# Layer 2 of a four-layer convolution kernel: the last half image cut in two quarters, and the half before it measured by ScalarE sums that GpSimd folds

## The chip, the cores and the metric

The kernel runs on one core of one Trainium2 chip. A core has a matrix engine (TensorE, PE in the profile, with its weight loads shown apart as PEld), a vector engine (VectorE, DVE), a scalar engine (ScalarE, ACT), GpSimd (POOL), and a queue engine (SyncE, SP) that issues transfers. Each engine works through its own list of instructions in order, and waits on semaphores for the others. The metric is the device time of one execution in microseconds. Before the change the median of three runs is 950.27 us (950.23 to 951.56).

## The reference, cut to what matters

The input is 16 images of 256 channels and 28 x 28 pixels. Four layers follow one another; the change is in layer 2, which consists of two binary convolutions with batch normalisations:

```python
out = batchnorm(x, g1, b1); out = binact(out)          # signs
out = prelu(binconv(out, w1, 1), a1)                   # first convolution, "l2b" below
out = batchnorm(out, g2, b2); out = binact(out)
out = prelu(binconv(out, w2, 1), a2)                   # second convolution, "l2c" below
out = batchnorm(out, g3, b3)
out = prelu(out + x, a3)
```

`batchnorm` takes the mean and the variance of each channel over all 16 images. So nothing behind such a normalisation can start before the last pixel of the last image has been convolved, activated and counted. Layers 0 and 1 come before (a binary convolution; a Winograd-like convolution with gates), layer 3 after (attention over the 784 pixels of each image).

## The kernel before, in words

The 256 channels are two groups of 128 partitions, called `mo` or `k` (0 and 1). An image is 784 values per partition and group; half an image is 14 rows, 392 values (`HN`), and a quarter is 7 rows, 196 values. Weights are plus and minus one. Two output channels are packed into one weight (`PACK`), so that one matmul computes both groups, and the result is split afterwards.

`sign_layer` (line 358) runs a binary convolution over a list of blocks `(image, first row, rows)`. Layer 2 uses `HALVES`, 32 blocks of 14 rows; layer 0 uses `PARTS`, which is the same list with its last block cut into two quarters of 7 rows. The order is written out by hand for PE, ACT, DVE and SP; GpSimd's instructions, and everything outside those blocks, are ordered by a planner. For block j it issues:

- `products(j)`: 18 matmuls (2 input groups x 3 rows x 3 columns of the kernel window) into one PSUM tile, line 378.
- the signs of the next image (ScalarE, line 1206), when a new image begins.
- `post(j-1)`: the activation and statistics of the block before, see below.
- `apart(j)`: ScalarE takes the packed product out of PSUM as int16 (line 394), and VectorE subtracts it to get the other channel (line 396). This pair waits for the matmuls of block j.
- the work that `post(j-1)` returned for ScalarE (`after`).

`post2.post` (line 1230) treats one block for the groups `mo` = 1 and 0. VectorE applies PReLU (line 1241) into the resident tile `pt`, and then collects count, mean and squared deviation with a statistics instruction (line 1249). For group 1 of every second of the first 22 blocks (`EARLY`), `by_sums` says that there is no statistics instruction: the PReLU instruction also gives the sum, and ScalarE gives the sum of squares around a base value (`square_p`, line 1260). Besides this, ScalarE squares the raw values for a range guard (`square`, line 1254, "doubts"); those of the last image are kept in `last_squares` and issued by `late_squares` after the layer.

`Moments` holds the statistics. `gather` (line 177) aggregates the first 22 blocks early; its result goes into the first three columns of `fin`. Each later block has six columns of `fin`, which VectorE fills. At the end a call (line 209) aggregates `fin` once per group. Then `sign_norm` (line 244, after l2b) or `norm` (line 212, after l2c) makes scale and shift of them with some ten tiny VectorE instructions and one square root on ScalarE.

After each convolution the code issues `keep_busy(n)` (line 476): n matmuls of 128x512 on a tile of zeros, which nobody reads. They are put into PE's list between the last real matmul and the next real one. Layer 2 uses 30 of them after l2b (line 1298) and 39 after l2c (line 1313). Behind those after l2b come the first matmuls of l2c, which need the signs of image 0 (ScalarE). Behind those after l2c come the first query and key matmuls of layer 3 (line 1454), which need image 0 normalised, added to the residual and activated (lines 1601 to 1608).

GpSimd has little to do around there: when the weights of l2b are no longer needed, it clears a tile of keys in their place (line 1417), and when l2c is over, it clears a few small tiles (lines 1410 to 1417).

Of the kernel before, what the change touches and what calls it, by code (L numbers as in the profile page):

```python
# [27 lines left out]
F32 = mybir.dt.float32  # L28
# [5 lines left out]
AF = mybir.ActivationFunctionType  # L34
ALU = mybir.AluOpType
# [4 lines left out]
P = 128  # L40
B = 16
S = 28
N = S * S
HN = N // 2
# [3 lines left out]
HALVES = [(j // 2, HR * (j % 2), HR) for j in range(2 * B)]  # L48

PARTS = HALVES[:-1] + [(B - 1, r, HR // 2) for r in (HR, HR + HR // 2)]  # L50
NB = len(PARTS)
IMAGES = [(i, 0, S) for i in range(B - 2)]
EARLY = 22
MC = 112
GN, GC = N // 4, MC // 4
NC_ = N // MC
# [29 lines left out]
def forward(ctx: ExitStack, tc: tile.TileContext, d: dict, out: bass.AP, careful: bool):  # L86
# [3 lines left out]
    nc = tc.nc  # L90
    V, A, T = nc.vector, nc.scalar, nc.tensor

    const = ctx.enter_context(tc.tile_pool(name="const", bufs=1))
    wpool = ctx.enter_context(tc.tile_pool(name="wpool", bufs=1))
    small = ctx.enter_context(tc.tile_pool(name="small", bufs=3))
# [7 lines left out]
    def pv(name):  # L103
        return vec[:, VECS.index(name), :]
# [20 lines left out]
    doubts = const.tile([P, 4 * NB + 10], F32, name="doubts")  # L125
# [9 lines left out]
    def tt(o, a, b, op):  # L135
        V.tensor_tensor(o, a, b, op)  # L136
        return o
# [17 lines left out]
    class Moments:  # L155


        def __init__(self, name, early, late, early_count, summed=False):
            self.parts = const.tile([P, 2, early, 6], F32, tag="parts", name=name + "_parts")
            self.summed = summed  # L160
            if summed:
                self.sums = const.tile([P, 2, early // 2], F32, tag="sums", name=name + "_sums")
                self.tot, self.base = (const.tile([P, n], F32, name=name + q) for n, q in ((3, "_tot"), (1, "_base")))
            self.fin = const.tile([P, 2, 3 + 6 * late], F32, name=name + "_fin")
            self.mv = const.tile([P, 2, 2], F32, name=name + "_mv")
            self.early, self.count, self.name = early, float(early_count), name

        def part(self, at, k):
            if at >= self.early:
                return self.fin[:, k, 6 * (at - self.early) + 3:][:, 0:6]  # L170
            return self.parts[:, k, at // 2 if self.summed and k == 1 else at, :]

        def by_sums(self, at, k):

            return self.summed and k == 1 and at < self.early and at % 2 == 1

        def gather(self):

            nc.gpsimd.memset(self.fin[:, :, 0:1], self.count)
            ps = [self.parts[:, k].rearrange("p c s -> p (c s)") for k in range(2)]  # L180
            if self.summed:
                h = self.early // 2
                t, tot, n = self.parts[:, 1, h, :], self.tot, float(h * HN)
                nc.gpsimd.memset(t[:, 0:1], n)
                V.tensor_reduce(tot[:, 0:2], self.sums, AX.X, ALU.add)
                V.tensor_scalar(t[:, 1:2], tot[:, 0:1], 1.0 / n, None, ALU.mult)
                tt(tot[:, 2:3], t[:, 1:2], self.base, ALU.add)
                tt(tot[:, 2:3], tot[:, 2:3], tot[:, 2:3], ALU.mult)
                V.scalar_tensor_tensor(t[:, 2:3], tot[:, 2:3], -n, tot[:, 1:2], ALU.mult, ALU.add)
                ps[1] = ps[1][:, 0:6 * h + 3]  # L190
            for k in range(2):
                V.bn_aggr(self.fin[:, k, 1:3], ps[k])
            V.tensor_scalar(self.fin[:, :, 2:3], self.fin[:, :, 2:3], self.count, None, ALU.mult)
# [160 lines left out]
    def first_part(block):  # L354

        return 2 * block[0] + (block[1] >= HR) + (block[1] > HR)
# [93 lines left out]
    def block_moments(name, blocks, summed=False):  # L450
        return Moments(name, EARLY, len(blocks) - EARLY, EARLY * HN, summed and not careful)

# [15 lines left out]
    with tc.tile_pool(name="ps_conv", bufs=3, space=PSUM) as psc, \  # L468
# [7 lines left out]
        def keep_busy(n):  # L476

            ps = pss.tile([P, 512], F32, tag="sm", name="unused")
            for _ in range(n):
                tc.keep_in_program_order(T.matmul(ps, lhsT=idle[:, 0:P], rhs=idle, start=True, stop=True))  # L480

        with tc.tile_pool(name="ph1", bufs=1) as ph:

            fpads = sign_pads(ph, "vs") if careful else sign_pads(const, None)
# [19 lines left out]
            def temp(tag):  # L504
                return ph.tile([P, HN if careful else N], F32, tag=tag, name=tag, bufs=2)
# [134 lines left out]
            w2a = packed_weights(wpool, tag="wa2")  # L640
# [7 lines left out]
            steps = [constants]  # L648
# [16 lines left out]
            mom = block_moments("l0", PARTS)  # L665
# [521 lines left out]
        with tc.tile_pool(name="ph2", bufs=1) as ph:  # L1187
# [37 lines left out]
            def post2(order, alpha, mom, doubt):  # L1225

                if careful:
                    beta = combine(mom.name + "_beta", alpha, -1.0, 1.0)

                def post(block, ab):  # L1230
                    i, r0, rows = block
                    at = first_part(block)
                    for mo in (0, 1) if careful else (1, 0):
                        y = ab[:, mo]
                        p = pt[order[i]][:, mo, r0 * S:(r0 + rows) * S]
                        if careful:
                            r = temp("t1")[:, :rows * S]
                            A.activation(r, y, AF.Relu, scale=-1.0)
                            V.scalar_tensor_tensor(p, r, beta[:, mo:mo + 1], y, ALU.mult, ALU.add)
                        else:  # L1240
                            V.scalar_tensor_tensor(  # L1241
                                p, y, alpha[:, mo:mo + 1], y, ALU.mult, ALU.max,
                                accum_out=mom.sums[:, 0, at // 2:at // 2 + 1] if mom.by_sums(at, mo) else None,
                            )
                        if mom.by_sums(at, mo):
                            by_sums = p
                            continue
                        for h, _, m in pieces(block):
                            V.bn_stats(mom.part(at + h, mo), p[:, h * HN:h * HN + m * S])
                        if mom.summed and (at, mo) == (0, 1):  # L1250
                            V.tensor_scalar(mom.base, mom.part(0, 1)[:, 1:2], -1.0, None, ALU.mult)

                    def square(h, m):
                        A.activation(
                            temp("t2")[:, :m * S], ab[:, 0, h * HN:h * HN + m * S], AF.Square, scale=SAFE**-0.5,
                            accum_out=doubt[:, at + h:at + h + 1],
                        )

                    def square_p():
                        A.activation(  # L1260
                            temp("t2")[:, :rows * S], by_sums, AF.Square, bias=mom.base,
                            accum_out=mom.sums[:, 1, at // 2:at // 2 + 1],
                        )

                    squares = [lambda h=h, m=m: square(h, m) for h, _, m in pieces(block) if not careful]
                    if mom.by_sums(at, 1):
                        squares.append(square_p)
                    if i < B - 1:
                        return squares
                    last_squares.extend(squares)  # L1270
                    return ()
                return post

            last_squares = []
# [15 lines left out]
            shifted = None  # L1290
            if not careful:
                shifted = ph.tile([P, 2, 2, S + 2, S + 2], SIGNS, name="shifted")
            mom = block_moments("l2b", HALVES, True)
            sign_layer(fpads, w2a, temp, room2, sign2a, post2(order, pv("a1"), mom, doubts[:, 2 * NB:3 * NB]), steps, mom, HALVES,
                       shifted=shifted, direct=4)
            late_squares()

            keep_busy(30)
            sg2, bg2 = sign_norm("l2b", mom, pv("g2"), pv("b2"), sf1)

            mom = block_moments("l2c", HALVES, True)
            sign_layer(
                fpads, w2b, temp, room2, lambda i, rows, out: sign2(pt[i], sg2, bg2, rows, out),
                post2(range(B), pv("a2"), mom, doubts[:, 3 * NB:4 * NB]), [], mom, HALVES, shifted=shifted,
            )
            late_squares()

            if careful:
                keep_busy(45)
                sg3, bg3 = norm("l2c", mom, pv("g3"), pv("b3"), sf2)  # L1310
                tt(bg3, bg3, cc, ALU.add)
            else:
                keep_busy(39)
                with tc.manual_schedule(engines={ET.DVE, ET.Activation}):
                    sg3, shift3 = norm("l2c", mom, pv("g3"), pv("b3"), sf2, late=True)
                    bg3 = shift3(b3c)
# [597 lines left out]
```

## Time and profile before

| what | value |
|---|---|
| median of three runs | 950.27 us |
| the profiled execution: time of its own | 949.96 us |
| its span, first to last instruction | 948.2 us |
| granted TensorE clock | 0.998 |
| busy: PE / DVE / ACT / POOL | 932.7 / 758.2 / 672.6 / 136.4 us |
| end of l2b, ScalarE begins to take out the last block | 558.93 us |
| first matmul of l2c | 565.21 us |
| end of l2c, ScalarE begins to take out the last block | 661.24 us |
| first matmul of layer 3 | 669.73 us |

Times inside the execution are microseconds from the start of the span. Engine times overlap; PE is busy nearly throughout, and in its busy time the unused matmuls of `keep_busy` are counted as well. The two stretches from 558.93 to 565.21 and from 661.24 to 669.73 are the ones in which the change takes place; in both of them PE does nothing that enters the result.

### The profile page before, as it was taken

The page shows a single profiled execution, that of the slowest core. Times are in us where ns is not written, and L with a number is a line of the kernel's source. Part 1 is how long each engine was busy: PE and PEld are TensorE (multiplying, and loading weights), DVE is VectorE, ACT ScalarE, POOL GpSimd, SP SyncE. Part 2 cuts the span into 40 slices and gives each one's busy share as a digit, 9 for nine tenths or more (in the row PEclk, how much of TensorE's full clock was granted, in tenths as well). Part 3 has the DMA queues.
Part 4 walks back from the last instruction along what each step waited for, and adds up shares of the span by engine and source line. Part 5 has one row for each costly group of instructions (what it writes and reads, how often), then busy time and mean ns, then how long its engine had stood idle before and what let it go on. Part 6 is the DMA issues. An engine that isn't in the chain of part 4 may idle for free.

```text
span 948.2 us, 14936 instructions
## 1 busy us (share of the span) xinstructions
PE 932.7 (98%) x5602; PEld 581.8 (61%) x5608; DVE 758.2 (80%) x1436; ACT 672.6 (71%) x1165; POOL 136.4 (14%) x145
## 2 busy tenths in 40 slices
PE   8999999999999999999999999999999999999996
PEld 4555678888888878887555555555444444444442
DVE  4777798999998899987788878889656768687765
ACT  6665568888888888865777756775766666676652
POOL 2001100000000000000000000000334353534431
PEclk9999999999999999999999999999999999999999
DMA  9888434445543444421555201111232434434212
GB/s 349 297 294 269 158 121 139 169 176 204 191 139 139 154 155 158 168 78 60 221 209 211 109 38 60 79 78 59 35 68 68 109 97 91 114 77 128 68 69 105
DMA packets 39332, 130.68 MB, mean 138 GB/s; under 512 B 4866, under 2 KB 16324, under 8 KB 39252
## 3 DMA queue, kind: packets, MB, share of 16 engines
q1 hardware_dynamic: 33332, 98.31, 28.9%
q0 software_dynamic: 5632, 30.54, 11.9%
q8 instruction: 45, 0.74, 0.3%
q10 hardware_dynamic: 288, 0.80, 0.2%
q14 instruction: 35, 0.29, 0.1%
HBM read 72.67 MB, written 32.11 MB: 111 GB/s over the span
## 4 chain that ended last, share of the span: by engine, by line
PE 95%; ACT 1%; DVE 1%; DMA 1%; SPq 1%; issue 0%; DVEq 0%; ACTq 0%
PE cv L378 30%; PE cv L784 29%; PE sc L1477 9%; PE av L1498 8%; PE cv L911 5%; PE mi L1454 5%; PE sm L1540 2%; PE unused L480 2%; PE mi L1558 2%; PE sm L1498 1%; DMA xs<-in_x_dram 1%; PE gate L879 1%; PE hid L687 1%; ACT es L1481 0%; SPq L271 0%
## 5 line engine op out<-in xcount | busy, mean ns | idle before, releaser
L784 PE MATMUL cv<-vs,w 128*128 128x392 f32 (+1 forms) x1296 | 272.5, 352 | 0.3 <-DVE vs L136 0.3
L378 PE MATMUL cv<-fpads,wpk 128*128 128x392 f16 (+1 forms) x1434 | 248.0, 329 | 1.2 <-DVE wpk L303 0.8
L378 PEld LDWEIGHTS <-wpk 128*128 128x128 f16 x1746 | 169.0, 97 | 124.3 <-issue 2.4
L784 PEld LDWEIGHTS cv<-vs,w 128*128 128x128 f32 x768 | 143.2, 190 | 6.2
L1481 ACT ACTIVATE es<-sc 128x784 f32<-128x784 f32 x112 | 87.3, 822 | 41.7 <-PE sc L1477 41.7
L784 PEld LDWEIGHTS <-w 128*128 128x128 f16 x768 | 69.4, 99 | 51.9 <-issue 9.1
L1477 PE MATMUL sc<-q,keyswa 64*128 64x392 f32 x448 | 89.9, 513 | 0.9 <-ACT es L1481 0.9
L1498 PE MATMUL av<-es,v 128*64 128x392 f32 x448 | 80.7, 499 | 0.0
L1241 DVE SCALAR_TENSOR_TENSOR p<-ab,vec 128x392 f32<-128x392 int16 x128 | 77.3, 616 | 0.0
L394 ACT ACTIVATE ab<-cv 128x392 int16<-128x392 f32 x64 | 31.8, 496 | 57.4 <-PE cv L378 54.5
L1491 POOL TENSOR_TENSOR sum<-sum,es 128x784 f32<-128x784 f32 x32 | 67.2, 2100 | 3.1 <-ACT es L1481 0.6
L1477 PEld LDWEIGHTS sc<-q,keyswa 64*128 64x128 f32 x448 | 38.9, 186 | 44.0 <-issue 17.1
L378 PE MATMUL cv<-shifted,wpk 128*128 128x392 f16 x312 | 60.2, 328 | 0.0
L784 PE MATMUL cv<-one_on,w 128*128 128x392 bf16 x240 | 59.5, 329 | 0.0
L1465 DVE COPY keyswa<-mi 64x392 f32<-64x392 f32 x31 | 16.3, 564 | 53.4 <-ACT q L1461 53.4
L1498 PEld LDWEIGHTS av<-es,v 128*64 128x64 f32 x448 | 29.4, 136 | 47.3 <-issue 47.0
L939 POOL DMA_DIRECT2D x2d<-x x16 | 8.6, 537 | 345.3 <-DVE x L933 284.9
L396 DVE SCALAR_TENSOR_TENSOR ab<-ab,cv 128x392 int16<-128x392 int16 x64 | 35.7, 558 | 27.8 <-ACT ab L394 27.5
L766 ACT CAST vs<-vs 128x840 fp32r<-128x840 bf16 x63 | 54.1, 883 | 2.5 <-DVE vs L136 2.5
L911 PE MATMUL cv<-z,fw 128*128 128x392 f32 x256 | 48.9, 342 | 0.1
L911 PEld LDWEIGHTS cv<-z,fw 128*128 128x128 f32 x256 | 46.1, 188 | 0.9 <-ACT z L903 0.9
L1454 PE MATMUL mi<-p,wqk 128*128 128x392 f32 x124 | 45.1, 506 | 0.1
(313 smaller groups left out, 1527.9 us busy)
## 6 DMA issues: line engine op xcount, KB each, us to landing
xs<-in_x_dram SPq DMA_DIRECT2D x30, 784.0 KB, 5.0
one_on<-vs SPq DMA_DIRECT2D x60, 209.8 KB, 3.0
x2d<-x POOLq DMA_DIRECT2D x16, 784.0 KB, 3.6
out_dram<-p SPq DMA_DIRECT2D x15, 784.0 KB, 3.7
shifted<-fpads SPq DMA_DIRECT2D x26, 449.8 KB, 2.7
p<-x2d POOLq DMA_DIRECT2D x14, 784.0 KB, 6.9
p<-x2d SPq DMA_DIRECT2D x13, 784.0 KB, 5.4
n0d<-n POOLq DMA_DIRECT2D x16, 392.0 KB, 4.4
```

Source lines behind the costliest of these rows:

```text
L378: T.matmul(pss[j][:, n // size if careful else h, :rows * S].rearrange("p (a b) -> p a b", b=S), lhsT=w[:, n, c, :], rhs=src[:, blocks[j][ ...
L394: A.activation(by_halves(ab[:, 1], blocks[j]), ps, AF.Copy, scale=1.0 / PACK)
L396: V.scalar_tensor_tensor(a, b, -PACK, ps, ALU.mult, ALU.add)
L766: copy(v, w)
L784: T.matmul(ps.rearrange("p (a b) -> p a b", b=S), lhsT=w[:, k, c, u, mo * P:(mo + 1) * P], rhs=one_on[:, u, k, :, 0:S] if moved and c == 1 ...
L911: T.matmul(ps[:, h, :HN], lhsT=w[:, k, mo * P:(mo + 1) * P], rhs=z2[b][:, k, h * HN:(h + 1) * HN], start=(k + i == 0), stop=(k + i == 2),)
L1241: V.scalar_tensor_tensor(p, y, alpha[:, mo:mo + 1], y, ALU.mult, ALU.max, accum_out=mom.sums[:, 0, at // 2:at // 2 + 1] if mom.by_sums(at, ...
L1454: T.matmul(ps[:, h, :HN], lhsT=wqk[:, k, :], rhs=x[b][:, k, h * HN:(h + 1) * HN], start=(k == 0), stop=(k == 1))
L1477: T.matmul(ps[:, h, :HN], lhsT=chunk[rows], rhs=qs[b][rows], start=True, stop=True)
L1481: A.activation(e, ps[:, :, :HN], AF.Exp, scale=0.125)
L1491: (V if late else nc.gpsimd).tensor_tensor(sums[b, late], sums[b, late], e, ALU.add)
L1498: T.matmul(ps[64 * h:64 * h + 64, :HN], lhsT=w, rhs=e[:, h, :], start=start, stop=stop)
```

## The change

Layer 2 now uses `PARTS`: its last block, 14 rows, becomes two quarters of 7 rows (numbers 31 and 32). The block ahead of them, the first half of the last image (number 30, `LATE`), gets no statistics instructions on VectorE. In their place, for both groups, the PReLU instruction gives a sum, and ScalarE squares the block around `base` with a sum (`square_p`), now issued right after the first quarter has been taken out. A new method `fold` makes count, mean and squared deviation of the four sums with six instructions on GpSimd, and puts them into columns 3 to 5 of `fin`. The base value is kept for both groups, and made after block 0 in one instruction. The unused matmuls are 26 in place of 30, and 35 in place of 39.

```diff
+LATE = 2 * B - 2
...
+                self.tot = const.tile([P, 3], F32, name=name + "_tot")
+                self.base = const.tile([P, 2, 1], F32, name=name + "_base")
+                self.late_sums = const.tile([P, 2, 2], F32, name=name + "_late")
-            self.fin = const.tile([P, 2, 3 + 6 * late], F32, name=name + "_fin")
+            self.fin = const.tile([P, 2, (0 if summed else 3) + 6 * late], F32, name=name + "_fin")
...
             if at >= self.early:
-                return self.fin[:, k, 6 * (at - self.early) + 3:][:, 0:6]
+                n = 6 * (at - self.early) + (3 if not self.summed else 6 if at < LATE else 0)
+                return self.fin[:, k, n:n + 6]
...
-            return self.summed and k == 1 and at < self.early and at % 2 == 1
+            return self.summed and (at == LATE or k == 1 and at < self.early and at % 2 == 1)
+        def sums_at(self, at, k):
+            if at == LATE:
+                return [self.late_sums[:, q, k:k + 1] for q in range(2)]
+            return [self.sums[:, q, at // 2:at // 2 + 1] for q in range(2)]
+        def fold(self):
+            g, n = nc.gpsimd, float(HN)
+            t, d = self.fin[:, :, 3:6], small.tile([P, 2], F32, tag="mv", name="fold")
+            (s, q), base = (self.late_sums[:, i] for i in range(2)), self.base[:, :, 0]
+            g.memset(t[:, :, 0:1], n)
+            g.tensor_scalar(t[:, :, 1], s, 1.0 / n, None, ALU.mult)
+            g.tensor_tensor(d, t[:, :, 1], base, ALU.add)
+            g.tensor_tensor(d, d, d, ALU.mult)
+            g.tensor_scalar(d, d, -n, None, ALU.mult)
+            g.tensor_tensor(t[:, :, 2], d, q, ALU.add)
...
-                                accum_out=mom.sums[:, 0, at // 2:at // 2 + 1] if mom.by_sums(at, mo) else None,
+                                accum_out=mom.sums_at(at, mo)[0] if mom.by_sums(at, mo) else None,
                             )
                         if mom.by_sums(at, mo):
-                            by_sums = p
+                            by_sums.append((mo, p))
                             continue
...
-                        if mom.summed and (at, mo) == (0, 1):
-                            V.tensor_scalar(mom.base, mom.part(0, 1)[:, 1:2], -1.0, None, ALU.mult)
+                        if mom.summed and (at, mo) == (0, 0):
+                            V.tensor_scalar(mom.base, mom.parts[:, :, 0, 1:2], -1.0, None, ALU.mult)
...
-                    def square_p():
+                    def square_p(mo, p):
                         A.activation(
-                            temp("t2")[:, :rows * S], by_sums, AF.Square, bias=mom.base,
-                            accum_out=mom.sums[:, 1, at // 2:at // 2 + 1],
+                            temp("t2")[:, :rows * S], p, AF.Square, bias=mom.base[:, mo], accum_out=mom.sums_at(at, mo)[1],
                         )
...
-                    if mom.by_sums(at, 1):
-                        squares.append(square_p)
+                    squares_p = [lambda s=s: square_p(*s) for s in by_sums]
                     if i < B - 1:
-                        return squares
+                        return squares + squares_p
                     last_squares.extend(squares)
-                    return ()
+                    return squares_p + [mom.fold] if at == LATE and squares_p else ()
...
-            mom = block_moments("l2b", HALVES, True)
+            mom = block_moments("l2b", PARTS, True)
...
-            keep_busy(30)
+            keep_busy(26)
...
-            mom = block_moments("l2c", HALVES, True)
+            mom = block_moments("l2c", PARTS, True)
...
-                keep_busy(39)
+                keep_busy(35)
```

The calls of `sign_layer` for l2b and l2c are given `PARTS` in place of `HALVES` too.

More of the change, by code (lines that the diff above doesn't have):

```diff
@@ L162, in __init__ @@
                 self.sums = const.tile([P, 2, early // 2], F32, tag="sums", name=name + "_sums")
-                self.tot, self.base = (const.tile([P, n], F32, name=name + q) for n, q in ((3, "_tot"), (1, "_base")))
-            self.fin = const.tile([P, 2, 3 + 6 * late], F32, name=name + "_fin")
+                self.tot = const.tile([P, 3], F32, name=name + "_tot")
+                self.base = const.tile([P, 2, 1], F32, name=name + "_base")
+                self.late_sums = const.tile([P, 2, 2], F32, name=name + "_late")
+            self.fin = const.tile([P, 2, (0 if summed else 3) + 6 * late], F32, name=name + "_fin")
             self.mv = const.tile([P, 2, 2], F32, name=name + "_mv")
@@ L186, in gather @@
                 V.tensor_scalar(t[:, 1:2], tot[:, 0:1], 1.0 / n, None, ALU.mult)
-                tt(tot[:, 2:3], t[:, 1:2], self.base, ALU.add)
+                tt(tot[:, 2:3], t[:, 1:2], self.base[:, 1], ALU.add)
                 tt(tot[:, 2:3], tot[:, 2:3], tot[:, 2:3], ALU.mult)
@@ L1232, in post @@
                     at = first_part(block)
+                    by_sums = []
                     for mo in (0, 1) if careful else (1, 0):
@@ L1292, in forward @@
                 shifted = ph.tile([P, 2, 2, S + 2, S + 2], SIGNS, name="shifted")
-            mom = block_moments("l2b", HALVES, True)
-            sign_layer(fpads, w2a, temp, room2, sign2a, post2(order, pv("a1"), mom, doubts[:, 2 * NB:3 * NB]), steps, mom, HALVES,
+            mom = block_moments("l2b", PARTS, True)
+            sign_layer(fpads, w2a, temp, room2, sign2a, post2(order, pv("a1"), mom, doubts[:, 2 * NB:3 * NB]), steps, mom, PARTS,
                        shifted=shifted, direct=4)
             late_squares()
-            keep_busy(30)
+            keep_busy(26)
             sg2, bg2 = sign_norm("l2b", mom, pv("g2"), pv("b2"), sf1)
-            mom = block_moments("l2c", HALVES, True)
+            mom = block_moments("l2c", PARTS, True)
             sign_layer(
                 fpads, w2b, temp, room2, lambda i, rows, out: sign2(pt[i], sg2, bg2, rows, out),
-                post2(range(B), pv("a2"), mom, doubts[:, 3 * NB:4 * NB]), [], mom, HALVES, shifted=shifted,
+                post2(range(B), pv("a2"), mom, doubts[:, 3 * NB:4 * NB]), [], mom, PARTS, shifted=shifted,
             )
```

## The prediction

> **What bounds the kernel now.** I read the page first: its busy times, and its chain of work that ended last.
>
> ```profile
> PE 932.7 (98%) x5602; PEld 581.8 (61%) x5608; DVE 758.2 (80%) x1436; ACT 672.6 (71%) x1165; POOL 136.4 (14%) x145
> ...
> PE 95%; ACT 1%; DVE 1%; DMA 1%; SPq 1%; issue 0%; DVEq 0%; ACTq 0%
> ```
>
> PE's list sets the time, so an edit counts only by moving a PE instruction. Then I asked for that chain around the ends of l2b and l2c, where the edits lie (start, length, piece):
>
> ```profile
> 558.95 6.42 PE unused L480 x29
> 565.37 9.68 PE cv L378 x57
> ...
> 661.26 8.38 PE unused L480 x38
> 669.64 0.09 issue
> 669.73 1.55 PE mi L1454 x4
> ```
>
> After l2b PE goes from the unused matmuls straight to real ones: the unused ones are the bound. The timeline shows five of them in 1.24 us, each 0.379 us long, so their pace is (1.24 - 0.379) / 4 = 0.215 us. The first sign of image 0 starts at 564.19 and takes some 0.74 us (564.93), the first matmul of l2c starts at 565.21: some 0.25 us of slack. After l2c the last unused matmul starts at 669.26, so the list would be free at 669.47, but the query matmul starts at 669.73: there the vector chain is the bound, by 0.26 us.
>
> The chain itself, VectorE's timeline at the end of l2b:
>
> ```profile
> 559.46 0.56 DVE L396 SCALAR_TENSOR_TENSOR ab<-ab,cv 128x392 int16<-128x392 int16 x1
> 559.94 0.62 DVE L1241 SCALAR_TENSOR_TENSOR p<-ab,vec 128x392 f32<-128x392 int16 x1
> 560.59 0.57 DVE L1249 BATCH_NORM_STATS2 l2b_fin<-p 128x6 f32<-128x392 f32 x1
> 561.08 0.61 DVE L1241 SCALAR_TENSOR_TENSOR p<-ab,vec 128x392 f32<-128x392 int16 x1
> 561.60 0.43 DVE L209 BATCH_NORM_AGGREGATE l2b_mv<-l2b_fin 128x2 f32<-128x63 f32 x1
> 561.95 0.51 DVE L1249 BATCH_NORM_STATS2 l2b_fin<-p 128x6 f32<-128x392 f32 x1
> 562.50 0.44 DVE L209 BATCH_NORM_AGGREGATE l2b_mv<-l2b_fin 128x2 f32<-128x63 f32 x1
> ```
>
> Starts give the pace: 0.48 us after line 396, 0.65 from PReLU to the statistics that need it, 0.49 from statistics to an independent instruction.
>
> Layer 0 of this same kernel already ends with two quarters, which prices them (ScalarE's timeline, then VectorE's):
>
> ```profile
> 104.40 0.50 ACT L394 ACTIVATE n<-cv 128x392 int16<-128x392 f32 x1 [2.56 <-PE cv L378]
> 105.95 0.33 ACT L394 ACTIVATE n<-cv 128x196 int16<-128x196 f32 x1 [1.05 <-PE cv L378]
> 107.50 0.33 ACT L394 ACTIVATE n<-cv 128x196 int16<-128x196 f32 x1 [1.22 <-PE cv L378]
> ...
> 107.86 0.36 DVE L396 SCALAR_TENSOR_TENSOR n<-n,cv 128x196 int16<-128x196 int16 x1 [0.39 <-ACT n L394]
> 108.26 0.63 DVE L660 BATCH_NORM_STATS2 l_fin<-n 128x6 f32<-128x196 int16 x2
> ```
>
> A quarter costs PE 1.55 us. A VectorE instruction of a quarter takes about 0.205 us less than one of a half: 0.35 against 0.56 (line 396), 0.356 against 0.558 (statistics).
>
> [...] 18 matmuls of 196 columns take 1.55 us (86 ns each), 18 of 392 take 2.93 to 2.98. [...] arithmetic on 22 columns takes 0.24 to 0.28 us and repeats every 0.32.
>
> **The change part by part**, on the times of the profiled execution.
>
> *PE.* Two quarters take 3.10 us in place of 2.93 to 2.98: +0.13 at each end. Four unused matmuls fewer: -4 x 0.215 = -0.86. If nothing else holds PE, its next real matmul comes 0.73 us earlier.
>
> *VectorE, block 30.* Two statistics instructions go (each some 0.49 of pace), and two PReLUs gain a read of the accumulator (0.08 us; in the trace the pace of such a PReLU is 0.54). In l2c: line 396 of block 30 at 658.85, PReLUs at 659.33 and 659.87, free at 660.41. The first quarter's products end at 658.29 + 1.55 = 659.84; taken out by ScalarE at about 660.2 to 660.3, ahead of 660.41. So VectorE goes on without a gap: line 396 of quarter 31 at 660.41, PReLU 660.70, statistics 661.14, PReLU 661.43, statistics 661.87, and line 396 of quarter 32 at 662.16. PE has ended at 661.39 and ScalarE has taken the block out by about 661.8, so a backlog of VectorE, not PE, starts the tail. That is 0.39 us later than before (661.77), and it eats much of the shorter tail. Without the removed statistics it would be another 0.9 us later. The tail: PReLU 662.45, statistics 662.89, PReLU 663.18, statistics 663.62, aggregation 664.02 against 664.64 before: 0.62 us earlier. The query matmuls need that chain, whose rest is unchanged: 669.73 - 0.62 = 669.11. The unused ones would let go at 669.47 - 0.73 = 668.74, so the chain stays the bound. **Gain after l2c: 0.62 us.**
>
> In l2b the same steps give line 396 of quarter 32 at 559.84, the aggregations at 561.18 and 561.87, the first sign at 563.57 (564.19 before), and a first possible matmul at about 564.35. PE's list gets there at 565.21 - 0.73 = 564.48. **Gain after l2b: 0.73 us**, with 0.1 us of slack left.
>
> *ScalarE.* Two squares of a half with accumulator (0.61 + 0.19, pace 0.60) stand between taking out quarters 31 and 32. In l2c, behind 660.0 to 660.3, they end at 661.57, when quarter 32 has been ready since 661.42; it is out at 661.8. VectorE's backlog to 662.16 hides this; without that cover it would cost 0.15. The guard's square of quarter 31 (0.33 + 0.19) may be put ahead as well, as that of block 30 is in the trace (557.13, ahead of the take-out at 558.93); then the tail starts 0.1 later. The three squares of the last image end ahead of the square root, as the two do now.
>
> *GpSimd.* No row has these six on two columns; the nearest are 0.24 to 0.28 us every 0.32, and at the low end a small memset at 0.10. So fold takes 0.6 to 1.9 us; I take 1.9 and let all six wait for ScalarE's second sum, at 661.57 in l2c: ready at 663.5, ahead of the aggregation at 664.02. In l2b: 559.25 + 1.9 = 561.2, just when the first aggregation wants it. If only the last instruction waits, it is ready 1.6 us earlier. Cost taken: nothing, hidden by the tail of quarter 32. No transfer is issued or moved, so SP's queue isn't touched; POOL's gets the six, near the 0.84 us memset of the keys at 558.96.
>
> *At nothing:* base for two groups still takes one tiny instruction (0.15 us), now one statistics instruction later and well ahead of the first square that reads it (575.48, in l2c); 66 columns in place of 63 to aggregate (the trace has 0.38 to 0.44 us for 63 and 0.41 to 0.45 for layer 0's 69).
>
> Sum: -0.73 - 0.62 = -1.35 us. Layer 3 is bound by PE, and its chain starts earlier by the same amount. The profiled execution took 949.96 (span 948.2 and 1.8 around it), so 948.6; it is 0.3 below the median, so from the median 950.27 I get **948.9 us**. What this kernel's measurement can tell from no change is about 0.2%, 1.9 us; the forecast lies inside that.
>
> **Rivals.**
>
> *A. Fold comes late, or ScalarE is out of order.* If in l2b fold stands behind the memset of the keys, which waits for the last matmul (559.05) and takes 0.84, it ends at 559.9 + 1.9 = 561.8, 0.6 after it is wanted; PE then resumes at 564.95, gain 0.26. With 0.1 to 0.2 lost on ScalarE at the other end the total is about -0.7: 949.6. For it: the memset's place in the trace. Against: most of fold needs only VectorE's sums, done by 558.2.
>
> *B. Slower: fold gates the statistics.* Fold and the statistics of quarter 31 write the same tile, `fin`. If VectorE's statistics are made to wait until fold has written, they start in l2c at 663.5 in place of 661.14; everything on VectorE behind them (line 396 of quarter 32, the tail) is 2.4 us late. The chain then loses 2.4 - 0.62 = 1.75 us after l2c, and after l2b, with its 0.25 of old slack, 1.5. Total +3.25: 953.5. It decides once fold ends over 0.6 us behind the point where the statistics are due; with a quick fold the total is near zero. Against it: the columns don't overlap, and the trace shows no waits between writers of different columns; but GpSimd hasn't written there late so far.
>
> *C. More gain.* If VectorE has no backlog, l2c's gain is limited by the unused matmuls: 669.73 - 668.74 = 0.99, total -1.72: 948.55. More than that the PE list doesn't give; over 1.9 is left to scatter and to something I don't see. Against it: VectorE's arithmetic above is tight.
>
> **How the numbers follow.** Forecast 0.68 (its own range 948.5 to 949.4), A 0.12, B 0.10 (of which 0.07 over 0.2%), C and beyond 0.10. Range 948.2 to 950.6: it takes in the forecast, A, C and B's mild end, and leaves out B's full loss and gains beyond the PE list. Faster by over 0.2%: 0.09, from the far side of C; slower: 0.07, from B; same: 0.84.
>
> **What would show it.** In the profile after: the first matmul of l2c near 564.5, straight behind the unused ones, with no idle of PE; the first query matmul near 669.1 less the 0.73 of l2b, about 668.4, with a small wait for VectorE ahead of it; line 396 of quarter 32 right behind the statistics of quarter 31, not waiting for ScalarE; aggregation not waiting for POOL. Wrong would be: a wait of VectorE on POOL, a take-out of quarter 32 later than VectorE's backlog, or l2c's gain taken back in layer 3 by a transfer or by ScalarE.

## The result, and the profile after

The changed kernel takes 949.08 us (median of 22 runs, 948.64 to 950.42), the kernel before beside it 950.32 us (22 runs, 950.08 to 952.04). The ratio is 0.9986 with a 95% interval of 0.998 to 0.9991: 1.3 us faster, between 0.9 and 1.9. That is less than the 0.2% (1.9 us) that the prediction names as the least to be told from no change, but the interval leaves out 1. The profiled execution took 949.33 us with a span of 947.5. Line numbers after the change are higher by 21 to 23 around here (378 is 400, 396 is 418, 1241 is 1264, 1249 is 1272, 1454 is 1475, 1477 is 1498).

The page of the kernel after, busy times:

```profile
PE 930.7 (98%) x5636; PEld 583.2 (62%) x5636; DVE 757.1 (80%) x1446; ACT 675.1 (71%) x1179; POOL 139.0 (15%) x157
```

PE still fills the span; PE and VectorE have a little less to do, ScalarE and GpSimd a little more. The chain of work that ended last, around the two ends (start, length, piece):

```profile
559.15 5.61 PE unused L502 x26
564.76 10.26 PE cv L400 x60
...
661.07 7.57 PE unused L502 x35
668.64 0.09 issue
668.73 1.55 PE mi L1475 x4
```

As before, the unused matmuls run into the next real work at both ends (with 0.09 us between at the second), but with 26 and 35 of them. VectorE's timeline at the end of l2b, from the second PReLU of block 30 on:

```profile
557.77 0.62 DVE L1264 SCALAR_TENSOR_TENSOR p<-ab,vec 128x392 f32<-128x392 int16 x1
558.32 0.08 DVE L1264 DVE_READ_ACCUMULATOR p<-ab,vec 128x1 f32 x1
558.32 0.35 DVE L418 SCALAR_TENSOR_TENSOR ab<-ab,cv 128x196 int16<-128x196 int16 x1
558.59 0.42 DVE L1264 SCALAR_TENSOR_TENSOR p<-ab,vec 128x196 f32<-128x196 int16 x1
559.04 0.37 DVE L1272 BATCH_NORM_STATS2 l2b_fin<-p 128x6 f32<-128x196 f32 x1
559.32 0.41 DVE L1264 SCALAR_TENSOR_TENSOR p<-ab,vec 128x196 f32<-128x196 int16 x1
559.76 0.37 DVE L1272 BATCH_NORM_STATS2 l2b_fin<-p 128x6 f32<-128x196 f32 x1
560.04 0.35 DVE L418 SCALAR_TENSOR_TENSOR ab<-ab,cv 128x196 int16<-128x196 int16 x1
...
561.36 0.45 DVE L231 BATCH_NORM_AGGREGATE l2b_mv<-l2b_fin 128x2 f32<-128x66 f32 x1
```

No line has a wait. VectorE works through quarter 31 and reaches quarter 32 (line 418 for the second time) at 560.04, though PE's last product started before 558.99, where the unused ones begin. Whether the new work on the other engines is in the way shows in ScalarE's and GpSimd's timelines of the same stretch:

```profile
557.73 0.33 ACT L416 ACTIVATE ab<-cv 128x196 int16<-128x196 f32 x1 [0.51 <-PE cv L400]
557.96 0.61 ACT L1283 ACTIVATE t<-p,l2b_base 128x392 f32<-128x392 f32 x1
...
558.56 0.61 ACT L1283 ACTIVATE t<-p,l2b_base 128x392 f32<-128x392 f32 x1
...
559.17 0.52 ACT L1277 ACTIVATE t<-ab 128x392 f32<-128x392 int16 x1
559.59 0.19 ACT L1277 ACTIVATION_READ_ACCUMULATOR t<-ab 128x1 f32 x1
559.68 0.31 ACT L416 ACTIVATE ab<-cv 128x196 int16<-128x196 f32 x1
```

```profile
558.49 0.23 POOL L193 TENSOR_SCALAR l2b_fin<-l2b_late 128x2 f32<-128x2 f32 x1 [20.88 <-DVE p L1264]
558.80 0.25 POOL L194 TENSOR_TENSOR fold<-l2b_fin,l2b_base 128x2 f32<-128x2 f32 x1
559.13 0.19 POOL L195 TENSOR_TENSOR fold<-fold 128x2 f32<-128x2 f32 x1
559.41 0.39 POOL L196 TENSOR_SCALAR fold<-fold 128x2 f32<-128x2 f32 x1
559.88 0.20 POOL L197 TENSOR_TENSOR l2b_fin<-fold,l2b_late 128x2 f32<-128x2 f32 x1
560.01 0.85 POOL L1438 MEMSET keyswa<- 128x896 f32 x1
```

ScalarE has quarter 32 out at 559.68 + 0.31 = 559.99, just 0.05 us before VectorE comes to it: the range guard's square of block 30 (line 1277) stands ahead of the take-out and uses up nearly all of the time that VectorE's backlog hides. Fold begins as soon as VectorE's sums are there, is done at 560.08, 1.28 us before the aggregation at 561.36, and writes `fin` while VectorE's statistics write other columns of it, without a wait on either side. (Its first instruction, which sets the count, isn't among these lines: it was done at 4.6 us.)

Two executions of one kernel can differ ahead of the ends already (ScalarE takes out block 30 of l2b at 556.21 us in the changed kernel's trace, at 555.85 in that of e10, the same kernel), so I measure each end by itself in the trace, from ScalarE's take-out of block 30: 556.00 and 556.21 in l2b, 658.32 and 658.13 in l2c, before and after. "First end" is from there to the first matmul of l2c; "to 2nd block" to ScalarE's take-out of the second block of l2c (571.58 and 571.05), which tells how much of it is kept. At the second end the columns go to the first query matmul and to the first matmul of attention scores (674.35 and 673.54) of layer 3. "Rest" is from that one to the first matmul of an output projection near the end (938.61 and 937.79). All kernels run, with the median of 13 to 22 runs, and that of the kernel before in the same comparison beside it:

| kernel | median us | beside it, before | first end | to 2nd block | to query | to scores | rest |
|---|---|---|---|---|---|---|---|
| before | 950.32 | | 9.21 | 15.58 | 11.41 | 16.03 | 264.26 |
| changed | 949.08 | 950.32 | 8.39 | 14.84 | 10.60 | 15.41 | 264.25 |
| e1: only fewer unused | 950.07 | 950.19 | 8.98 | 15.46 | 11.06 | 15.99 | 264.26 |
| e2: changed, all unused | 950.20 | 950.19 | 9.25 | 15.62 | 11.46 | 16.08 | 264.26 |
| e3: changed, no sums | 951.23 | 950.19 | 9.53 | 16.02 | 11.62 | 16.54 | 264.27 |
| e4: changed, no quarters | 950.04 | 950.19 | 9.01 | 15.50 | 11.16 | 16.09 | 264.26 |
| e5: fold, 3 more | 948.93 | 950.18 | 8.39 | 14.84 | 10.60 | 15.43 | 264.25 |
| e6: fold, 8 more | 951.67 | 950.18 | 10.39 | 18.52 | 11.29 | 16.21 | 264.26 |
| e7: changed, still fewer unused | 948.94 | 950.18 | 8.34 | 14.83 | 10.50 | 15.42 | 264.24 |
| e8: quarter by sums | 948.52 | 950.18 | 8.51 | 15.00 | 10.00 | 14.92 | 264.24 |
| e9: e8, fold in one piece | 948.12 | 950.17 | 8.03 | 14.51 | 10.00 | 14.92 | 264.22 |
| e10: changed again | 948.89 | 950.17 | 8.38 | 14.82 | 10.59 | 15.41 | 264.25 |

The first matmul of l2c comes 9.21 - 8.39 = 0.82 us earlier, but the second block only 0.74. The fourth matmul is the first that reads input group 1, and it waits: in the changed kernel it starts 0.25 us behind the third (564.94 and 565.19), in the kernel before 0.17. ScalarE's sign of that group is done at 563.77 + 1.37 = 565.14. At the second end the change saves 0.81 to the query matmul, but only 16.03 - 15.41 = 0.62 to the scores; what lies behind the scores takes the same time in all twelve traces. Sum: 0.74 + 0.62 = 1.36 us from the ends, 1.24 from the medians. Some traces also show a loss inside l2c: between its blocks 29 and 30, 2.99 us apart in the kernel before and in e7, the changed kernel, e10 and e5 take 0.35, 0.16 and 0.07 us more. In the first of them PE waits 0.20 us for a DMA there; whether the change has a part in this isn't shown.

### The profile page after: what moved, and what is told of

It reads as the page before. It is cut to its first block, busy times and chain, and to the rows that moved or that the text cites. A ratio compares the mean times of both kernels' runs of the same rounds, so it can differ in the third digit from the quotient of the medians.

```text
span 947.5 us, 15043 instructions
## 1 busy us (share of the span) xinstructions
PE 930.7 (98%) x5636; PEld 583.2 (62%) x5636; DVE 757.1 (80%) x1446; ACT 675.1 (71%) x1179; POOL 139.0 (15%) x157
## 4 chain that ended last, share of the span: by engine, by line
PE 94%; DMA 1%; ACT 1%; DVE 1%; SPq 1%; issue 0%; DVEq 0%; ACTq 0%
PE cv L400 29%; PE cv L806 29%; PE sc L1498 8%; PE av L1519 8%; PE cv L933 5%; PE mi L1475 5%; PE sm L1561 2%; PE mi L1579 2%; PE unused L502 2%; PE sm L1519 1%; DMA xs<-in_x_dram 1%; PE gate L901 1%; PE hid L709 1%; DMA shifted<-fpads 1%; SPq L293 0%
## 5 line engine op out<-in xcount | busy, mean ns | idle before, releaser
L400 PEld LDWEIGHTS <-wpk 128*128 128x128 f16 x1782 | 171.5, 97 | 123.2 <-issue 3.1
L1264 DVE SCALAR_TENSOR_TENSOR p<-ab,vec 128x392 f32<-128x392 int16 (+1 forms) x132 | 78.0, 605 | 0.0
L416 ACT ACTIVATE ab<-cv 128x392 int16<-128x392 f32 (+1 forms) x66 | 32.1, 486 | 56.3 <-PE cv L400 53.4
L400 PE MATMUL cv<-shifted,wpk 128*128 128x392 f16 (+1 forms) x324 | 60.6, 322 | 0.2 <-DMA shifted<-fpads 0.2
L418 DVE SCALAR_TENSOR_TENSOR ab<-ab,cv 128x392 int16<-128x392 int16 (+1 forms) x66 | 36.0, 546 | 27.7 <-ACT ab L416 27.3
```

The lines of the kernel that those rows point to most:

```text
L400: T.matmul(pss[j][:, n // size if careful else h, :rows * S].rearrange("p (a b) -> p a b", b=S), lhsT=w[:, n, c, :], rhs=src[:, blocks[j][ ...
L416: A.activation(by_halves(ab[:, 1], blocks[j]), ps, AF.Copy, scale=1.0 / PACK)
L418: V.scalar_tensor_tensor(a, b, -PACK, ps, ALU.mult, ALU.add)
L1264: V.scalar_tensor_tensor(p, y, alpha[:, mo:mo + 1], y, ALU.mult, ALU.max, accum_out=mom.sums_at(at, mo)[0] if mom.by_sums(at, mo) else None,)
```

## The experiments

Theory after the result: each end of layer 2 has two things that can hold PE, the list of unused matmuls and the chain VectorE–ScalarE–VectorE behind the last block; they lie within some tenths of a microsecond of each other, and the three parts of the change (fewer unused, quarters, sums) each move only one. So none is worth much alone. The rivals give the gain to one part.

**e1: only the unused matmuls.**

```diff
-            keep_busy(30)
+            keep_busy(26)
...
-                keep_busy(39)
+                keep_busy(35)
```

> The kernel before with 26 and 35 unused matmuls in place of 30 and 39, nothing else changed. Theory (both ends are bound by the unused matmuls, with the vector chain close behind): the first matmul of the second convolution comes 0.2 us earlier, when the first signs are ready, and the first query matmul 0.4 us earlier, when the activation is ready: -0.6 us in all. Rival (the unused matmuls alone make the gain): -0.86 us at each end, -1.7 us. Rival (the vector chain bounds the second end, as forecast): -0.2 and 0, -0.2 us.

Measured: 950.07 us beside 950.19, ratio 1.0003 (0.9994 to 1.0011). PE's timeline of e1:

```profile
565.04 2.15 PE L378 MATMUL cv<-fpads,wpk 128*128 128x392 f16 x11 [0.47 <-ACT fpads L1206]
...
669.33 1.55 PE L1454 MATMUL mi<-p,wqk 128*128 128x392 f32 x4 [0.62 <-DVE p L1608]
```

At both ends PE now stands idle and waits for the chain. The first end gains 0.23 us, of which 0.12 is left at the second block. The query matmul comes 0.35 earlier, the scores only 0.04: PE waits for the second half of image 0 instead, which the chain delivers when it did before. My theory's -0.6 missed: it counted the first matmul at each end, where little is decided. The total (-0.12) is nearest to that of the rival which repeats the forecast, -0.2, but that rival had no gain at the query matmul, and there are 0.35 us. The intervals of e1, e2 and e4 reach some 0.8 us to each side, more than what separates the theories here, so for these three runs the traces decide and not the totals.

**e2: the change with all unused matmuls.** The edit is the reverse of e1's, on the changed kernel.

> The changed kernel with 30 and 39 unused matmuls as before. Theory: PE's list is longer by what the quarters cost, 0.1 us at each end, and the shorter vector chain is worth nothing: +0.2 us against the kernel before (+1.5 against the changed one). Rival (the vector chain bounds the second end, as forecast): the query matmul still gains some 0.1 to 0.6 us, so -0.1 to -0.5 us against before.

Measured: 950.20 us beside 950.19, ratio 0.9998 (0.999 to 1.0007); the ends are 0.04 and 0.05 longer than before. The shorter chain alone is worth nothing, at either end. The rival, which was my forecast's reading of the second end, predicted a gain of 0.1 to 0.6 at the query matmul; there is none.

**e3: the quarters and fewer unused matmuls, with VectorE's statistics for block 30.**

```diff
-            return self.summed and (at == LATE or k == 1 and at < self.early and at % 2 == 1)
+            return self.summed and k == 1 and at < self.early and at % 2 == 1
```

The columns of `fin` are laid out as in the kernel before, to take block 30's statistics.

> The changed kernel, but the half ahead of the quarters has its statistics from VectorE as before: no sums, no fold. Theory (VectorE's backlog sets the tail, and the two statistics instructions are worth 0.9 us of it): both ends are bound by the vector chain, which is 0.9 us later than in the changed kernel: +0.2 us at the first end and 0 at the second, against the kernel before; so about +0.2 us against before, +1.4 against the changed one. Rival (the quarters bring the gain, the sums none): as the changed kernel, -1.3 us.

Measured: 951.23 us beside 950.19, ratio 1.0011 (1.0004 to 1.0017): slower than before, by 1.04 us at the medians. The theory has the sign and the reason, not the size: its ends are 0.32 and 0.51 longer than before, and 1.14 and 1.13 longer than in the changed kernel. VectorE's timeline of e3, the take-up of quarter 32 and the first aggregation:

```profile
561.25 0.34 DVE L418 SCALAR_TENSOR_TENSOR ab<-ab,cv 128x196 int16<-128x196 int16 x1
...
562.57 0.46 DVE L231 BATCH_NORM_AGGREGATE l2b_mv<-l2b_fin 128x2 f32<-128x69 f32 x1
```

Counted from the take-out of block 30 (556.26), VectorE comes to quarter 32 after 4.99 us, against 3.83 in the changed kernel. So the two removed statistics instructions carry 1.16 us, not the 0.9 that I took from their pace to an independent successor. What counts is the pair: from a PReLU to its statistics 0.65 us and on to the next PReLU 0.48, together 1.13, against 0.55 from a PReLU with accumulator to the next. That is 0.58 each.

**e4: the sums and fewer unused matmuls, without quarters.** The two `PARTS` of layer 2 are `HALVES` again.

> The changed kernel with the last half of the last image as one block again, the sums of the half ahead and the fewer unused matmuls kept. Theory (the sums only empty VectorE's list in front of the last block; without the quarters VectorE waits for the matmuls of the last block anyway): as with the fewer unused matmuls alone, -0.6 us against before. Rival (the sums bring the gain by themselves): -1.3 us.

Measured: 950.04 us beside 950.19, ratio 1.0 (0.9991 to 1.0008). The ends are those of e1 (9.01 against 8.98, 16.09 against 15.99). VectorE's timeline of e4:

```profile
558.15 0.08 DVE L1264 DVE_READ_ACCUMULATOR p<-ab,vec 128x1 f32 x1
559.56 0.56 DVE L418 SCALAR_TENSOR_TENSOR ab<-ab,cv 128x392 int16<-128x392 int16 x1 [1.33 <-ACT ab L416]
```

The time that the sums free turns into a wait of 1.33 us for the last block. Its total is again e1's, for e1's reason. Taken at their medians, of the three parts, each two without the third give +0.01 (e2), +1.04 (e3) and -0.15 us (e4); all three give -1.24.

**e5 and e6: a longer fold.** On the changed kernel, n = 3 or 8 more instructions in the chain of fold:

```diff
             g.tensor_scalar(d, d, -n, None, ALU.mult)
+            for _ in range(3):
+                g.tensor_scalar(d, d, 1.0, None, ALU.mult)
             g.tensor_tensor(t[:, :, 2], d, q, ALU.add)
```

> The changed kernel with three more GpSimd instructions (a multiplication by one) in the chain of fold. Theory (only the last aggregation waits for fold, with 1.3 us to spare at the first end and 1.9 at the second): fold ends 0.9 to 1.4 us later and the time is that of the changed kernel, within 0.1 us. Rival (fold also holds the statistics of the quarters, which write the same tile): +0.9 to +1.4 us at each end.

> The changed kernel with eight more GpSimd instructions in the chain of fold. Theory: fold ends 2.5 to 3.8 us later, which passes the spare 1.3 and 1.9 us; the aggregation waits for GpSimd, and the time rises by 1.2 to 2.5 us at the first end and 0.4 to 1.9 at the second, +1.6 to +4.4 us against the changed kernel. Rival (fold is hidden whatever its length): 0.

Measured: e5 948.93 us, ratio 0.9985 (0.9979 to 0.9992), both ends as in the changed kernel: the cover is there. e6 951.67 us, ratio 1.002 (1.0013 to 1.0026), 2.7 us above the changed kernel. Its profiled execution (953.46) was longer than its median, inside l2c: behind PE's 1.84 us of idle time 21 matmuls took 5.49 us from the first start to the last end (566.80 to 572.29), 20 of them 3.64 us in the changed kernel (564.60 to 568.24), and the second block was taken out 8.13 us behind the first matmul in place of 6.45 (18.52 - 10.39, 14.84 - 8.39). So I use its two ends only: +2.00 and +0.80 to the scores. VectorE's and GpSimd's timelines of e6, first end:

```profile
561.23 0.41 DVE L1266 SCALAR_TENSOR_TENSOR p<-ab,vec 128x196 f32<-128x196 int16 x1
563.60 0.45 DVE L233 BATCH_NORM_AGGREGATE l2b_mv<-l2b_fin 128x2 f32<-128x66 f32 x1 [1.96 <-POOL l2b_fin L199]
```

```profile
560.08 2.53 POOL L198 TENSOR_SCALAR fold<-fold 128x2 f32<-128x2 f32 x8
562.54 0.85 POOL L1440 MEMSET keyswa<- 128x896 f32 x1
563.36 0.21 POOL L199 TENSOR_TENSOR l2b_fin<-fold,l2b_late 128x2 f32<-128x2 f32 x1
```

Only the aggregation waits; the statistics in front of it don't. And here the planner has put the clearing of the keys between the last two instructions of fold, 0.8 us of the loss at this end. That is rival A of the prediction; in the changed kernel it doesn't occur: the memset starts at 560.01 us, behind the start of fold's last instruction at 559.88.

**e7: fewer unused matmuls than the change has**, 22 and 31.

> The changed kernel with 22 and 31 unused matmuls. Theory (the vector chain stands right behind the unused matmuls at both ends): the first end gains 0.1 us at most, the second 0.2: 0 to -0.3 us against the changed kernel, with PE idle 0.6 to 0.8 us ahead of the next real matmul. Rival (the unused matmuls are still the only bound): -0.86 us at each end, -1.7 us.

Measured: 948.94 us beside 950.18, ratio 0.9986 (0.998 to 0.9993), the time of the changed kernel. PE's timeline of e7 shows the wait that was said:

```profile
564.59 2.66 PE L400 MATMUL cv<-fpads,wpk 128*128 128x392 f16 x14 [0.66 <-ACT fpads L1228]
...
668.37 1.55 PE L1475 MATMUL mi<-p,wqk 128*128 128x392 f32 x4 [0.87 <-DVE p L1629]
```

So in the changed kernel both counts stand right at the chain: four fewer bring nothing.

**e8: the first quarter by sums as well.** If VectorE's backlog holds the tail, taking more statistics from it in front of quarter 32 must help. Both groups of quarter 31 give sums, ScalarE squares them, one fold treats both blocks (five GpSimd instructions on four columns), the guard's squares of the last image are issued behind all of that, and the unused matmuls are 23 and 32.

```diff
-            return self.summed and (at == LATE or k == 1 and at < self.early and at % 2 == 1)
+            return self.summed and (at in (LATE, LATE + 1) or k == 1 and at < self.early and at % 2 == 1)
...
-                    return squares_p + [mom.fold] if at == LATE and squares_p else ()
+                    return squares_p + ([mom.fold] if at == LATE + 1 and squares_p else [])
...
-            keep_busy(26)
+            keep_busy(23)
...
-                keep_busy(35)
+                keep_busy(32)
```

> An attempt at a faster kernel: the first quarter is measured by ScalarE's sums too (for both groups), one fold for both blocks, the range guard's squares of the last image behind all of this on ScalarE, 23 and 32 unused matmuls. Theory (VectorE's backlog sets the tail): VectorE takes up the last quarter 0.5 us earlier, as soon as ScalarE has it out, and the chain is 0.5 us shorter at each end: -0.9 to -1.1 us against the changed kernel, -2.3 against before. Rival (ScalarE becomes the bound: fold comes after the aggregation wants it, or the guard's squares delay the square root): 0 to +0.5 us against the changed kernel.

Measured: 948.52 us beside 950.18, ratio 0.9985 (0.9978 to 0.9992). The second end is 0.49 shorter than in the changed kernel, as the theory says; at the first end the theory missed, for it is 0.12 longer. The edit also moves the guard's squares, so the gain isn't shown to be VectorE's alone. GpSimd's and VectorE's timelines of e8, first end:

```profile
559.70 0.30 POOL L202 TENSOR_TENSOR fold<-fold 128x4 f32<-128x4 f32 x1
559.94 0.84 POOL L1447 MEMSET keyswa<- 128x896 f32 x1
560.74 0.20 POOL L203 TENSOR_TENSOR fold<-fold,l2b_less 128x4 f32<-128x4 f32 x1
561.02 0.20 POOL L204 TENSOR_TENSOR l2b_fin<-fold,l2b_late 128x4 f32<-128x4 f32 x1
```

```profile
561.25 0.44 DVE L238 BATCH_NORM_AGGREGATE l2b_mv<-l2b_fin 128x2 f32<-128x63 f32 x1 [0.59 <-POOL l2b_fin L204]
```

Rival A again: the memset cuts fold in two, and the aggregation waits.

**e9: the same with fold in one piece**, and the changed kernel once more beside it (e10).

```diff
-    for t in keys + [vt]:
-        nc.gpsimd.memset(t, 0.0)
+    for t in keys:
+        with tc.issue_after(first_fold.ins):
+            nc.gpsimd.memset(t, 0.0)
+    nc.gpsimd.memset(vt, 0.0)
```

`first_fold` is the last instruction of fold in l2b.

> The kernel with the first quarter by sums, but GpSimd clears the keys behind the whole of fold (in its trace the planner had put the 0.84 us memset between the third and the fourth instruction of fold, and VectorE's aggregation waited 0.59 us for GpSimd at the first end). Theory: fold ends when ScalarE's last sum is there, the aggregation no longer waits, the first matmul of the second convolution comes 0.6 us earlier, the second end stays: -0.6 us against the kernel with the first quarter by sums, -1.1 against the changed kernel, -2.3 against before. Rival (the aggregation then waits for ScalarE's sums of the first quarter, or PE for its unused matmuls): -0.2 us at most against the kernel with the first quarter by sums.

> The changed kernel itself once more, beside the attempt: -1.25 us against before.

Measured: e9 948.12 us (947.78 to 949.88), ratio 0.998 (0.9973 to 0.9987); e10 948.89 us (948.61 to 949.51), ratio 0.9986 (0.9979 to 0.9993); before 950.17. GpSimd's and VectorE's timelines of e9:

```profile
561.85 0.37 POOL L206 TENSOR_TENSOR l2b_fin<-fold,l2b_late 128x4 f32<-128x4 f32 x1
562.15 1.62 POOL L1450 MEMSET keyswa<- 128x896 f32 x2
```

```profile
561.75 0.40 DVE L1275 SCALAR_TENSOR_TENSOR p<-ab,vec 128x196 f32<-128x196 int16 x1
562.25 0.44 DVE L240 BATCH_NORM_AGGREGATE l2b_mv<-l2b_fin 128x2 f32<-128x63 f32 x1
```

The first end gains 0.48 us on e8 rather than 0.6: the aggregation starts 0.50 behind the PReLU, where the changed kernel needs 0.32 (561.04 to 561.36), so fold, which now ends at 562.22 behind ScalarE's last sum, still holds it by some 0.2 (an estimate from these two gaps). e9 is the fastest kernel here, 0.8 us below the changed one at the medians of the same comparison; the two ratio intervals overlap a little, and the ends say the same from the traces (0.36 and 0.49 shorter, 0.85 in sum).

## Why the prediction was right

It forecast 948.9 us and -1.35 us; measured are 949.08 and -1.24 (by the ratio -1.3). The mechanism, a backlog of VectorE and a list of unused matmuls that must be shortened together, is what the runs show; that the total is so near is in part luck, as two points below say. Point by point:

- **VectorE's backlog sets the tail: right, to 0.03 us.** Counted from the take-out of block 30 in l2b, the forecast had quarter 32 taken up after 3.84 us and the aggregation after 5.18; the trace has 3.83 and 5.15. e3 shows what the backlog costs without the sums, e4 that the sums are idle time without the quarters.
- **The first end is bound by the unused matmuls: right for the first matmul**, and e7 shows how close the chain is behind it (0.05). Forecast 0.73, measured 0.82. Part of the difference is the price of the quarters on PE: I took 1.55 us each from layer 0; in l2b they start 1.52 us apart (555.95, 557.47, 558.99), 3.04 in all where I had 3.10. The step looked at the first sign alone and counted 0.1 us of slack; the second sign, for the fourth matmul, comes 0.08 late. So 0.74 are kept, and that this is the forecast's 0.73 is luck.
- **The second end: the amount right, the step wrong.** The prediction read the 0.26 us ahead of the query matmul as a wait for the vector chain. e1 leaves the chain alone and takes four unused matmuls, and the query matmul comes 0.35 us earlier: in the kernel before the unused ones held it. What I took for the end of the list is the start of the last unused matmul plus one pace (669.47); its own end is 669.24 + 0.38 = 669.62. The traces show the hold directly, as a wait for a semaphore on PE's queue of weight loads, ahead of the query product (before, then changed; ns):

```profile
L1454 PEldq EVENT_SEMAPHORE  x1: 397/397/397, 669.3 to 669.3; - x1
...
L1475 PEldq EVENT_SEMAPHORE  x1: 152/152/152, 668.5 to 668.5; - x1
```

  Both waits end 0.05 us behind the last unused matmul (669.62 and 668.62). In e2 the weight load follows the end of that matmul as closely (669.88 and 669.96); in e1, with the list four shorter, it comes 0.59 us behind it (668.71 and 669.30), so there the list no longer holds it. What the step overlooked beside this is that PE's next stop counts, the second half of image 0. VectorE is done with it at 671.45 and 670.70; counted from the take-out of block 30 that is 13.13 and 12.57 us, so the chain brings it 0.56 us earlier, a little less than the forecast 0.62. In the kernel before, the list had been some 0.05 behind the chain there as well (e1 gains 0.04 to the scores). Both together make the 0.62 that reached the scores: the same number as the forecast, by luck. The 0.81 that the query matmul gained was given back by 0.19 there.
- **ScalarE's squares are hidden: right, barely.** The guard's square went ahead of the take-out, as was said to be possible, and 0.05 us of cover was left. It was block 30's square, and not quarter 31's.
- **Fold is hidden: right.** Without the memset of the count it took 1.59 us, in the range of 0.6 to 1.9, and only its last instruction needs ScalarE. The spare is 1.28 us at the first end; e5 stays inside it, e6 passes it.
- **Rival B fell**: fold and the statistics write one tile at the same time without a wait, in the changed kernel and in e6. **Rival A** didn't happen here but is real: the memset cuts fold in two in e6 and e8, and VectorE's aggregation waits 1.96 and 0.59 us for GpSimd there. **Rival C** asked for no backlog; the backlog was there.
- The removed statistics were priced at 0.9 us and carry 1.16 (e3). The forecast's total didn't rest on that figure, since the chain was counted instruction by instruction.

## What to carry to other kernels

Where filler work and a dependent chain end at nearly the same time, price both, and expect parts of a change to be worth nothing alone and something together. Follow the chain past the first instruction that moves: part of a gain at the first consumer is given back if the second one waits for something of its own, as it did at both ends here (0.08 and 0.19 us). And when a small helper engine takes over work that is on the path, look at what its planner may put in the middle of it.

## What the runs showed of the hardware

- Ahead of the query product the weight load started 0.08 and 0.07 us after the last unused matmul had ended in the profile (669.62 to 669.70 before, 668.62 to 668.70 after), behind the semaphore wait shown above. At the first end, in the kernel before, the weight load of l2c's first matmul came while the last unused matmul still ran (564.99, its end at 565.37), and the profile has no such wait there. From the start of the last unused matmul to the next real one it took 0.49 us (669.24 to 669.73) at the one end, and 0.22 (564.99 to 565.21) at the other.
- In e6 PE stood idle for 1.84 us ahead of l2c. Behind that its matmuls started 0.26 us apart on average up to 572.29 (21 in 5.49 us, the last taking 0.33), against 0.17 in the changed kernel (20 in 3.64 us), and the second block was taken out 8.13 us behind the first matmul. In e3 and e7, with 0.98 and 0.66 us idle at the same place, it was 6.49 us in both (16.02 - 9.53, 14.83 - 8.34), against 6.45 in the changed kernel. Whether the length of the idle time decides it, and where between 0.98 and 1.84 us, these runs don't show.
- The five arithmetic instructions of fold, on two columns, took GpSimd 0.19 to 0.39 us each in the changed kernel; the same multiplication eight times in a row took 2.53 us in e6, 0.32 each.
- In the changed kernel a VectorE PReLU with accumulator and its independent successor started 0.55 us apart at 392 columns (557.22, 557.77, 558.32); in e3 it was 1.13 us from a PReLU past its statistics to the next instruction (558.41, 559.06, 559.54).
